# A graph network layer on Trainium2: other rules for when gathers are issued, in six stretches of the edge loop

## The chip, the core and the metric

The kernel runs on one core of a Trainium2 chip. A core has five engines, each with its own instruction queue: TensorE (PE in the profile; its weight loads are PEld), VectorE (DVE), ScalarE (ACT), GpSimd (POOL) and SyncE (SP). They meet only at semaphores. PE writes to the accumulators (PSUM), DVE and ACT take results from there, and DMA transfers move data between the device's memory and the on-chip memory. A gather here is an indirect DMA that POOL issues: it reads 128 row numbers and fetches 128 rows of 256 floats.

The metric is device time in microseconds (us); the shorter, the better. Beside the timed runs there is one profiled execution, with a record of every instruction.

## The reference

Nodes N = 6250 with D = 256 features, E = 206250 edges sorted by target, 64 features and one polarity per edge. Cut to what matters:

```python
h = relu(layernorm(x))
e = relu(raw @ W_e1.T + b_e1) @ W_e2.T + b_e2          # per edge
edge_emb = (e * (clip(edge_attr[:, 0:1], 0, 1) + 0.01)) @ W_le.T + b_le
msg  = relu(h[src] + edge_emb)
aggr = segment_sum(msg, dst, num_segments=6250)
o = (h + aggr) @ W_g1.T + b_g1
o = layernorm(o) * ln_g + ln_b
x = x + relu(o) @ W_g2.T + b_g2
```

## The kernel before

The matrices W_e2 and W_le are multiplied once into `wc_s`, so an edge needs two matmul layers. The kernel first makes `hb_d`, the normalised node rows plus b_le, in the device's memory. Then one long loop, written out instruction by instruction in this order (a manual schedule, nothing is moved by a planner), goes over the edges.

The edges are cut in tiles of 128. Two tiles are a **unit** (806 units, index `u`), four tiles a block, two blocks (four units) a **pair** (202 pairs). Six blocks are a group with one accumulator `pd` for the sums. For unit u:

- `edge_part(u)` (matmuls of L255): the second layer on PE into a PSUM tile `pz`, one of 7; DVE adds the bias into `msg` (L260).
- `whole(u)`: DVE multiplies by the edge's polarity and adds the gathered row into the gather's own buffer `hg` (L530, two instructions per unit); ACT takes the relu (L532).
- once per pair, when u % 4 is 1, `turn_of`: the first layer of a later pair (L233 on PE, L241 on ACT), then `sums` (`add_up`, L540): PE adds the finished `hg` of a pair into `pd` with 0/1 matrices `sel`, and frees their buffers; then the next load of edge features on SP.

There are 16 `hg` buffers of one unit. Gathers can't start before `hb_d` is written, so the loop begins with PE 22 units ahead: `made`, the number of units that went through `whole`, stands `LEAD - u // SHRINK` units behind u, 22 at the start and 1 at the end. When a group is complete, ACT copies `pd` (L546) and the work on the nodes follows in small pieces that `due` puts between the units (L161 to L188, L591 to L613).

What sets the order of the gathers: at each unit, after `forward(u)`, `ask` lets the number of asked units grow to `4 * summed + 12` plus 1, 2, 3 or 4, by the unit's place in the pair. For each new unit DVE copies its two columns of row numbers from `src_s` into a small tile `idx` (L500), then POOL gets the two gathers (L511). A gather waits for its `idx` copy, for the sums that free its buffer, and for the gather eight before it to have landed. The first 16 units are asked before the loop; on DVE their copies stand behind the two instructions that clip the polarities (L410, L411) and ahead of the cast of `dst_f` (L642).

Of the kernel before, what the change touches and what calls it, by code (L numbers as in the profile page):

```python
# [9 lines left out]
F32 = mybir.dt.float32  # L10
I32 = mybir.dt.int32
# [6 lines left out]
P = 128  # L18
# [10 lines left out]
S = 4  # L29
L = 6  # L30
W = 32
# [10 lines left out]
SHRINK = 36  # L42
HG = 16
TURN = 1
CH = 4
AHEAD = 10
assert DEG * N == E and NF * GE + S * P >= E
# [2 lines left out]
def group_of(b):  # L50
    return b // L


def blocks_of(g):
    return range(g * L, min((g + 1) * L, NB))
# [9 lines left out]
def groups_of(w):  # L65
    return [g for g in range(NG) if w in windows_of(g)]


def chunks():

    t = 0
    while t < NW:
        n = min(CH, N // P - t)
        if n <= 0:
# [17 lines left out]
def gnn_kernel(ctx: ExitStack, tc: tile.TileContext, x, src_c, dst_c, dst_r, pol_c, raw_t, w_e1t, w_e2,  # L92
               w_let, w_g1t, w_g2t, vec_c, row_v, x_t, out):
    nc = tc.nc

    const = ctx.enter_context(tc.tile_pool(name="const", bufs=1))
# [16 lines left out]
    wc_s = const.tile([P, 2, D], F32, name="wc_s")  # L113
    bc_s = const.tile([P, 2, D], F32, name="bc_s")
    src_s = const.tile([P, NT], I32, name="src_s")
# [82 lines left out]
    NU = 2 * NB  # L198
    fast = ExitStack()
    fast.enter_context(tc.manual_schedule())  # L200
    with fast:
# [8 lines left out]
        raw, sel, e1, hg, msg, ms = {}, {}, {}, {}, {}, {}  # L210

        pd = psd.tile([P, 2, D], F32, name="pd")

        def ps():
            return psz.tile([P, 2, D], F32, name="pz")
# [28 lines left out]
        def plain(u):  # L244

            return u < LEAD and u % 3 == 1

        def edge_part(u):

            b, v = divmod(u, 2)  # L250
            pz = ps()
            for i in range(2):
                k = (2 * v + i) * P
                for c in range(2):
                    nc.tensor.matmul(pz[:, i, :], e1[b][:, c, k:k + P], wc_s[:, c, :], start=c == 0, stop=c == 1)  # L255
            msg[u] = msg_p.tile([P, 2, D], F32, name="msg")
            if plain(u):
                nc.scalar.activation(msg[u], pz, AF.Copy)
            else:
                nc.vector.tensor_add(msg[u], pz, bc_s)  # L260
            if v == 1:
                e1.pop(b)

        sums = lambda: None

        def turn_of(q):

            if q + 2 < NP:
                first_layer(q + 2)
            sums()  # L270
            load_pair(q + 4)

        def forward(u):

            edge_part(u)
            if u % 4 == TURN:
                turn_of(u // 4)
# [30 lines left out]
        with tc.tile_pool(name="p1", bufs=4) as p1, tc.tile_pool(name="p1x", bufs=11) as p1x:  # L308
# [4 lines left out]
            def load_rows(k, halves=1):  # L313
                if k < len(parts):
                    t0, p, t = parts[k]
                    xts[k] = p1x.tile([P, CH, D], F32, name="xt")
                    h = t // halves
# [4 lines left out]
            def stats(k, i0, i1):  # L322
                t0, p, t = parts[k]
                if i0 == 0:
                    mvs[k] = p1.tile([P, CH, 2], F32, name="mvx")
                for i in range(i0, min(i1, t)):
                    row_stats(p1, p, 1, lambda _: xts[k][:p, i, :], mvs[k][:, i:i + 1, :])

            def root(k):
                t0, p, t = parts[k]  # L330
                nc.scalar.activation(rs_s[:p, t0:t0 + t], mvs[k][:p, :t, 1], AF.Sqrt, bias=eps_t[:p])

            def nodes_out(k):
# [6 lines left out]
                for i in range(t):  # L340
                    nc.scalar.activation(xt[:p, i, :], xt[:p, i, :], AF.Relu, bias=nm_s[:p, t0 + i:t0 + i + 1],  # L341
                                         scale=rs_s[:p, t0 + i:t0 + i + 1])
                hb = p1.tile([P, CH, D], F32, name="hb")
                for i in range(t):
# [40 lines left out]
            for k in range(len(parts) + 1):  # L385
# [9 lines left out]
                if k < len(parts):  # L395
                    stats(k, 2, CH)
                    root(k)
# [3 lines left out]
                for _ in range((k > 0) + (k > 2 and k % 3 > 0)):  # L401
                    u = next(units, None)
# [82 lines left out]


        with tc.tile_pool(name="hg", bufs=HG) as hg_p, tc.tile_pool(name="ms", bufs=5) as ms_p, \
                tc.tile_pool(name="sel2", bufs=9) as sel2_p, tc.tile_pool(name="nd", bufs=3) as nd, tc.tile_pool(name="idx", bufs=HG) as idx_p:
            idx = {}
            asked = 0  # L490
            got = 0
            made = 0
            summed = 0

            def ask(last):

                nonlocal asked
                while asked < min(NU, last):
                    idx[asked] = idx_p.tile([P, 2], I32, name="idx")
                    nc.vector.tensor_copy(idx[asked], src_s[:, 2 * asked:2 * asked + 2])  # L500
                    asked += 1
                gathers()

            def gathers():
                nonlocal got
                while got < asked:
                    u = got
                    got += 1
                    hg[u] = hg_p.tile([P, 2, D], F32, name="hg")
                    for i in range(2):  # L510
                        nc.gpsimd.indirect_dma_start(  # L511
                            out=hg[u][:, i, :], out_offset=None, in_=hb_d,
                            in_offset=bass.IndirectOffsetOnAxis(ap=idx[u][:, i:i + 1], axis=0))

            def select(g):

# [7 lines left out]
            def whole(u):  # L524

                m = msg.pop(u)
                if plain(u):
                    nc.vector.tensor_add(m, m, bc_s)
                for i in range(2):
                    nc.vector.scalar_tensor_tensor(hg[u][:, i, :], m[:, i, :], pol_s[:, 2 * u + i:2 * u + i + 1],  # L530
                                                   hg[u][:, i, :], op0=ALU.mult, op1=ALU.add)
                nc.scalar.activation(hg[u], hg[u], AF.Relu)  # L532

            def add_up(b):

                g = group_of(b)
                k = b - g * L
                for j in range(S):
                    m = hg[2 * b + j // 2]
                    nc.tensor.matmul(pd[j * W:(j + 1) * W, g % 2, :], sel[g][:, k * S + j, :], m[:, j % 2, :],  # L540
                                     start=k == 0, stop=b == blocks_of(g)[-1])
                hg.pop(2 * b)
                hg.pop(2 * b + 1)
                if b == blocks_of(g)[-1]:
                    ms[g] = ms_p.tile([P, D], F32, name="ms")
                    nc.scalar.activation(ms[g], pd[:, g % 2, :], AF.Copy)  # L546
                    sel.pop(g)
                    for w in range(NW):
                        if groups_of(w)[-1] == g:
                            late.pop(w)()  # L550
                        elif groups_of(w)[-1] == g + 1 < NG - 1:
                            late[w] = node_work(w)

            def add_pairs(last=False):

                nonlocal summed
                while summed < NP and min(4 * summed + 4, NU) < made + last:
                    for b in (2 * summed, 2 * summed + 1):
                        if b < NB:
                            add_up(b)  # L560
                            if b % L == 0 and group_of(b) + 2 < NG:
                                at(now + 2, lambda g=group_of(b) + 2: select(g))
                    summed += 1
# [3 lines left out]
            now = 0  # L567
# [65 lines left out]
            def due():  # L633

                fns = todo.pop(now, deque())
                if fns:
                    fns.popleft()()
                if fns:
                    todo.setdefault(now + 1, deque()).extendleft(reversed(fns))

            ask(HG)
            nc.vector.tensor_copy(dst_f, dst_f.bitcast(I32))  # L642
            sums = add_pairs
            for i, fn in enumerate((first_rows, rows_of_edges, lambda: select(0), lambda: select(1), row_numbers,
# [6 lines left out]
            for u in range(LEAD, NU):  # L651
                now = u
                forward(u)

                ask(4 * summed + HG - 4 + (u - TURN) % 4 + 1)
                while made < u + 1 - max(LEAST, LEAD - u // SHRINK):
                    whole(made)
                    made += 1
                due()
                if u == NU - 10:  # L660
                    for w in range(NW):
                        if groups_of(w)[-1] == NG - 1:
                            late[w] = node_work(w, True)
                if u == LEAD + 60:
                    flag = nc.values_load(bad_i[0:1, 0:1], min_val=0, max_val=3 * P)
# [4 lines left out]
            while todo:  # L670
                now = min(todo)
# [169 lines left out]
```

## Time and profile before

Three runs: 2218.32 us median (2217.36 to 2218.54).

| what | us |
|---|---|
| profiled execution | 2216.99 |
| its span, first to last instruction | 2215.3 |
| PE busy | 2190.5 |
| POOL busy, of it 1612 gathers of L511 | 1647.5, 1611.8 |
| DVE busy, of it 806 copies of L500 | 1535.6, 155.1 |
| ACT busy | 1064.2 |
| first gather starts, last gather starts (from the span's start) | 67.87, 2185.32 |

A row of the costliest groups has the line, the engine, the operation, the output and the inputs by the program's names, how often, then the busy time and the mean of one in ns, then the idle time of the engine just ahead of these instructions with what ended most of it. The view of waits has one row per pair of waiter and reason: the total, how often, the longest. A reason is the event that came last before the start, so a row names what finished last, which need not be what held the engine. "issue" is time in which the engine waited for nothing that the profile shows. In the timeline a line has the start, the duration, the engine, and in brackets the idle time before it. A gather's duration on POOL is that of its issue; the data lands later.

### The profile page before, as it was taken

Reading aid. Unit: us, or ns where it says so; the run is one execution under the profiler, and the core shown is the slowest. Engines: PE = TensorE matmul, PEld = TensorE weight load, DVE = VectorE, ACT = ScalarE, POOL = GpSimd, SP = SyncE. Lnnn points to the kernel's source line nnn. Section 1 sums busy time; section 2 is a strip of 40 time slices with the busy share of each in tenths; the row PEclk is TensorE's granted clock in tenths of the full one; section 3 lists DMA queues with packets and bytes.
Section 4 is the critical chain, followed back from the end, with each engine's and each line's share of the span. In section 5 each row is a group of like instructions: output and inputs, shape, how many; then the busy total and the mean of one; then the engine's idle time right before and its main releaser. Section 6 shows DMA issues by size and latency. Waiting matters only on the chain.

```text
span 2215.3 us, 35590 instructions
## 1 busy us (share of the span) xinstructions
PE 2190.5 (99%) x12360; PEld 1583.1 (71%) x12360; DVE 1535.6 (69%) x4083; ACT 1064.2 (48%) x1895; POOL 1647.5 (74%) x1674
## 2 busy tenths in 40 slices
PE   8999999999999999999999999999999999999997
PEld 6667777777777777777777776777777777777775
DVE  7786667677676666667667666766676667666766
ACT  7444454444444444444444445454444444454443
POOL 5777777777777777777777777777777777777773
PEclk9999999999999999999999999999999999999999
DMA  9444554444444444544444444444344344444442
GB/s 307 149 135 121 152 145 132 132 133 141 148 135 126 138 146 129 154 131 136 141 143 129 150 127 142 133 145 136 115 146 146 118 130 147 140 141 130 138 135 61
DMA packets 156083, 309.23 MB, mean 140 GB/s; under 512 B 33183, under 2 KB 77944, under 8 KB 155896
## 3 DMA queue, kind: packets, MB, share of 16 engines
q0 software_dynamic: 77376, 211.39, 32.2%
q1 hardware_dynamic: 77384, 92.24, 13.3%
q10 hardware_dynamic: 1136, 3.27, 0.4%
q8 instruction: 98, 1.61, 0.3%
q14 instruction: 89, 0.73, 0.1%
HBM read 293.92 MB, written 12.85 MB: 138 GB/s over the span
## 4 chain that ended last, share of the span: by engine, by line
PE 94%; DMA 2%; DVE 1%; issue 1%; ACT 0%; POOL 0%; SPq 0%; POOLq 0%; DVEq 0%; ACTq 0%
PE pz L255 62%; PE pz L233 17%; PE pd L540 9%; PE pz L611 3%; PE pz L183 2%; PE pz L161 2%; DMA hg<-hb_d,idx 1%; PE pz L173 0%; DVE hg L530 0%; POOL hg L511 0%; DMA raw<-in_raw_t_dram 0%; ACT e L241 0%; DVE msg L260 0%; DMA wle_s<-in_w_let_dram 0%; ACT hg L532 0%
## 5 line engine op out<-in xcount | busy, mean ns | idle before, releaser
L511 POOL DMA_INDIRECT hg<-hb_d,idx x1612 | 1611.8, 1000 | 512.6 <-issue 195.0
L255 PE MATMUL pz<-wc_s,e 128*128 128x256 f32 x6448 | 1479.1, 383 | 2.3 <-DVE msg L260 2.3
L255 PEld LDWEIGHTS pz<-wc_s,e 128*128 128x128 f32 x6448 | 1202.1, 190 | 239.2 <-issue 46.1
L532 ACT ACTIVATE hg<-hg 128x512 f32<-128x512 f32 x806 | 511.2, 634 | 1009.9 <-DVE hg L530 1005.4
L260 DVE TENSOR_TENSOR msg<-pz,bc_s 128x512 f32<-128x512 f32 x799 | 550.5, 689 | 601.2 <-PE pz L255 598.5
L530 DVE SCALAR_TENSOR_TENSOR hg<-msg,pol_s,hg 128x256 f32<-128x256 f32 x1612 | 707.2, 480 | 20.9 <-DMA hg<-hb_d,idx 19.6
L241 ACT ACTIVATE e<-pz,vecs 128x512 f32<-128x512 f32 x799 | 483.2, 686 | 97.3 <-PE pz L233 96.2
L233 PE MATMUL pz<-raw,we_s 64*128 64x512 f32 x1612 | 403.2, 617 | 5.5 <-DMA we_s<-in_w_e1t_dram 5.0
L233 PEld LDWEIGHTS pz<-raw,we_s 64*128 64x128 f32 x1612 | 139.8, 186 | 167.7 <-issue 135.2
L540 PE MATMUL pd<-hg,sel 128*32 128x256 f32 x3224 | 215.0, 385 | 4.1 <-ACT ms L546 4.1
L540 PEld LDWEIGHTS pd<-hg,sel 128*32 128x32 f32 x3224 | 84.4, 109 | 187.7 <-issue 134.8
L500 DVE COPY idx<-src_s 128x2 int32<-128x2 int32 x806 | 155.1, 197 | 0.0
L611 PEld LDWEIGHTS pz<-s,ms 128*128 128x128 f32 x560 | 70.1, 192 | 5.2 <-ACT ms L546 1.7
L611 PE MATMUL pz<-s,ms 128*128 128x128 f32 (+1 forms) x560 | 70.9, 275 | 1.7 <-ACT ms L546 1.5
L520 DVE TENSOR_TENSOR sel<-iota_w,rel 128x768 f32<-128x768 f32 x68 | 64.0, 941 | 0.0
L345 POOL TENSOR_TENSOR hb<-xt,rows_b 128x256 f32<-128x256 f32 (+1 forms) x49 | 34.2, 729 | 25.3 <-ACT xt L341 17.1
L183 PE MATMUL pz<-wg_s,nT 128*128 128x256 f32 (+1 forms) x196 | 50.3, 380 | 0.0
L161 PE MATMUL pz<-wg_s,hT 128*128 128x256 f32 (+1 forms) x196 | 50.1, 379 | 0.0
L601 DVE TENSOR_TENSOR hT<-hT,stb 128x256 f32<-128x256 f32 (+1 forms) x98 | 41.3, 421 | 1.7
L183 PEld LDWEIGHTS pz<-wg_s,nT 128*128 128x128 f32 (+1 forms) x196 | 36.9, 190 | 5.8 <-PE pd L540 0.4
L161 PEld LDWEIGHTS pz<-wg_s,hT 128*128 128x128 f32 (+1 forms) x196 | 37.1, 190 | 5.1
L176 ACT ACTIVATE nT<-pz,vecs 128x128 f32<-128x128 f32 (+1 forms) x98 | 38.8, 446 | 0.6 <-PE pz L173 0.6
(77 smaller groups left out, 359.4 us busy)
## 6 DMA issues: line engine op xcount, KB each, us to landing
raw<-in_raw_t_dram SPq DMA_DIRECT2D x202, 256.0 KB, 4.5
hg<-hb_d,idx POOLq DMA_INDIRECT x1612
stb<-st_d SPq DMA_DIRECT2D x49, 128.0 KB
hb_d<-hb SPq DMA_DIRECT2D x12, 512.0 KB
xt<-in_x_dram SPq DMA_DIRECT2D x48, 128.0 KB
hT<-in_x_t_dram SPq DMA_DIRECT2D x48, 128.0 KB, 4.0
out_dram<-ot SPq DMA_DIRECT2D x48, 128.0 KB, 2.0
xt<-in_x_dram SPq DMA_DIRECT2D x11, 512.0 KB, 8.9
```

The lines of the kernel that those rows point to most:

```text
L161: nc.tensor.matmul(ph[:n, 0, :], aT[:, c, :n], wg1_s[:, c, :], start=c == 0, stop=c == 1)
L183: nc.tensor.matmul(po[:n, 0, :], nT[:, c, :n], wg2_s[:, c, :], start=c == 0, stop=c == 1)
L233: nc.tensor.matmul(pe[s, c], we1_s[s * F:(s + 1) * F, c * P:(c + 1) * P], raw[q][s * F:(s + 1) * F, :], start=True, stop=True)
L241: nc.scalar.activation(e1[b][:, c, :], pe[s, c], AF.Relu, bias=be1_s[:, c:c + 1])
L255: nc.tensor.matmul(pz[:, i, :], e1[b][:, c, k:k + P], wc_s[:, c, :], start=c == 0, stop=c == 1)
L260: nc.vector.tensor_add(msg[u], pz, bc_s)
L500: nc.vector.tensor_copy(idx[asked], src_s[:, 2 * asked:2 * asked + 2])
L511: nc.gpsimd.indirect_dma_start(out=hg[u][:, i, :], out_offset=None, in_=hb_d, in_offset=bass.IndirectOffsetOnAxis(ap=idx[u][:, i:i + 1], a ...
L530: nc.vector.scalar_tensor_tensor(hg[u][:, i, :], m[:, i, :], pol_s[:, 2 * u + i:2 * u + i + 1], hg[u][:, i, :], op0=ALU.mult, op1=ALU.add)
L532: nc.scalar.activation(hg[u], hg[u], AF.Relu)
L540: nc.tensor.matmul(pd[j * W:(j + 1) * W, g % 2, :], sel[g][:, k * S + j, :], m[:, j % 2, :], start=k == 0, stop=b == blocks_of(g)[-1])
L611: nc.tensor.matmul(pa[:, c, :n], ms[g][:, c * P:(c + 1) * P], box["sel2"][i][:, :n], start=i == 0, stop=i == len(gs) - 1)
```

## The change

A table `STEPS` cuts the loop into six stretches by pair number (below 37, 70, 103, 136, 169, and the rest). A row has: how far the gathers may be asked at each of the four places in a pair; how many units back lies the unit whose matmuls the first gather of a call waits for (None: no such wait); whether at the first place it waits for the last sums instead; the columns of an idle memset on POOL (0: none) and for every how many units it is issued; and whether second gathers wait for the first half of the same unit's matmuls.

The copies `idx` are gone in all stretches: the gathers read their row numbers straight from `src_s`. The memsets write a tile `idle_t` that nobody reads. `edge_part` and `add_up` keep the matmuls that the gathers may wait for. The gathers now wait for: eight gathers back, their buffer, and what the table says. The stretch is chosen by the current unit; the units asked in it are some 12 to 16 units past the last summed one. The order of the instructions on PE, ACT and SP is the same as before; on DVE it is the same but for the copies.

```diff
@@ -42,6 +42,18 @@
+STEPS = (
+    (37, (1, 2, 3, 4), 0, False, 0, 1, True),
+    (70, (4, 4, 4, 4), None, False, 400, 1, False),
+    (103, (4, 4, 4, 4), None, False, 800, 4, False),
+    (136, (2, 2, 4, 4), 0, True, 0, 1, False),
+    (169, (4, 4, 4, 4), None, False, 1280, 4, False),
+    (999, (4, 4, 4, 4), 0, True, 0, 1, False),
+)
@@ -252,7 +264,8 @@
             for i in range(2):
                 k = (2 * v + i) * P
                 for c in range(2):
-                    nc.tensor.matmul(pz[:, i, :], e1[b][:, c, k:k + P], wc_s[:, c, :], start=c == 0, stop=c == 1)
+                    z = nc.tensor.matmul(pz[:, i, :], e1[b][:, c, k:k + P], wc_s[:, c, :], start=c == 0, stop=c == 1)
+                zs.setdefault(u, []).append(z)
             msg[u] = msg_p.tile([P, 2, D], F32, name="msg")
             if plain(u):
                 nc.scalar.activation(msg[u], pz, AF.Copy)
@@ -261,6 +274,9 @@
             if v == 1:
                 e1.pop(b)
 
+        zs = {}
+        last_sums = None
+        idle_t = const.tile([P, 1280], F32, name="idle_t")
         sums = lambda: None
 
         def turn_of(q):
@@ -485,32 +501,34 @@
 
 
         with tc.tile_pool(name="hg", bufs=HG) as hg_p, tc.tile_pool(name="ms", bufs=5) as ms_p, \
-                tc.tile_pool(name="sel2", bufs=9) as sel2_p, tc.tile_pool(name="nd", bufs=3) as nd, tc.tile_pool(name="idx", bufs=HG) as idx_p:
-            idx = {}
-            asked = 0
+                tc.tile_pool(name="sel2", bufs=9) as sel2_p, tc.tile_pool(name="nd", bufs=3) as nd:
             got = 0
             made = 0
             summed = 0
 
-            def ask(last):
-
-                nonlocal asked
-                while asked < min(NU, last):
-                    idx[asked] = idx_p.tile([P, 2], I32, name="idx")
-                    nc.vector.tensor_copy(idx[asked], src_s[:, 2 * asked:2 * asked + 2])
-                    asked += 1
-                gathers()
-
-            def gathers():
+            def step(q):
+                return next(s[1:] for s in STEPS if q < s[0])
+
+            def gathers(last, behind=None, half=None):
+
                 nonlocal got
-                while got < asked:
+                while got < min(NU, last):
+                    cols, every = step(now // 4)[3:5]
+                    if cols and got % every == 0:
+                        nc.gpsimd.memset(idle_t[:, :cols], 0.0)
                     u = got
                     got += 1
                     hg[u] = hg_p.tile([P, 2, D], F32, name="hg")
                     for i in range(2):
-                        nc.gpsimd.indirect_dma_start(
+                        g = nc.gpsimd.indirect_dma_start(
                             out=hg[u][:, i, :], out_offset=None, in_=hb_d,
-                            in_offset=bass.IndirectOffsetOnAxis(ap=idx[u][:, i:i + 1], axis=0))
+                            in_offset=bass.IndirectOffsetOnAxis(ap=src_s[:, 2 * u + i:2 * u + i + 1], axis=0))
+                        if i and half is not None:
+                            behind = half
+                        if behind is not None:
+                            tc.add_manual_dep(g.ins, behind.ins.name, mybir.DependencyInfo(
+                                mybir.DependencyClass.Sync, mybir.DependencyReason.DATA), reason="gathers in step with PE")
+                            behind = None
 
             def select(g):
 
@@ -533,11 +551,12 @@
 
             def add_up(b):
 
+                nonlocal last_sums
                 g = group_of(b)
                 k = b - g * L
                 for j in range(S):
                     m = hg[2 * b + j // 2]
-                    nc.tensor.matmul(pd[j * W:(j + 1) * W, g % 2, :], sel[g][:, k * S + j, :], m[:, j % 2, :],
+                    last_sums = nc.tensor.matmul(pd[j * W:(j + 1) * W, g % 2, :], sel[g][:, k * S + j, :], m[:, j % 2, :],
                                      start=k == 0, stop=b == blocks_of(g)[-1])
                 hg.pop(2 * b)
                 hg.pop(2 * b + 1)
@@ -638,7 +657,7 @@
                 if fns:
                     todo.setdefault(now + 1, deque()).extendleft(reversed(fns))
 
-            ask(HG)
+            gathers(HG)
             nc.vector.tensor_copy(dst_f, dst_f.bitcast(I32))
             sums = add_pairs
             for i, fn in enumerate((first_rows, rows_of_edges, lambda: select(0), lambda: select(1), row_numbers,
@@ -652,7 +671,10 @@
                 now = u
                 forward(u)
 
-                ask(4 * summed + HG - 4 + (u - TURN) % 4 + 1)
+                ask, ahead, by_sums, _, _, halves = step(u // 4)
+                k = (u - TURN) % 4
+                behind = last_sums if by_sums and k == 0 and last_sums else None if ahead is None else zs[u - ahead][1]
+                gathers(4 * summed + HG - 4 + ask[k], behind, zs[u - ahead][0] if halves else None)
                 while made < u + 1 - max(LEAST, LEAD - u // SHRINK):
                     whole(made)
                     made += 1
```

## The prediction

> **What bounds the kernel now.** I read the page first: the shares of the engines, the chain that ended last, and the costliest groups.
>
> ```profile
> PE 2190.5 (99%) x12360; PEld 1583.1 (71%) x12360; DVE 1535.6 (69%) x4083; ACT 1064.2 (48%) x1895; POOL 1647.5 (74%) x1674
> ...
> PE 94%; DMA 2%; DVE 1%; issue 1%; ACT 0%; POOL 0%; SPq 0%; POOLq 0%; DVEq 0%; ACTq 0%
> ...
> L511 POOL DMA_INDIRECT hg<-hb_d,idx x1612 | 1611.8, 1000 | 512.6 <-issue 195.0
> ```
>
> PE is on the path for 94% of the span. POOL looks free at 74%, but its row says otherwise: 512.6 us of idle time over 1612 gathers is 0.318 us before each. So I asked for POOL's own waits in the first part of the loop, 68 to 1300 us (reason: total us, times, longest):
>
> ```profile
> POOL hg L511 <- issue: 121.0, 397, 0.3
> POOL hg L511 <- DVE hg L530: 50.3, 165, 0.3
> POOL hg L511 <- DVE idx L500: 25.1, 64, 6.0
> POOL hg L511 <- ACT hg L532: 18.6, 61, 0.3
> ```
>
> Every pause but one is 0.3 us, whatever engine is named. That is the fixed gap of one gather after another; the named engine only happened to finish inside it. The one exception is the 6.0 us ahead of the first gather. In the timeline of POOL and of DVE around 1014 us:
>
> ```profile
> 1014.23 0.95 POOL L511 DMA_INDIRECT hg<-hb_d,idx  x1 [0.30 <-PE pz L233]
> 1015.49 0.94 POOL L511 DMA_INDIRECT hg<-hb_d,idx  x1 [0.31 <-DVE hg L530]
> 1016.73 0.95 POOL L511 DMA_INDIRECT hg<-hb_d,idx  x1 [0.30 <-issue]
> 1017.98 0.95 POOL L511 DMA_INDIRECT hg<-hb_d,idx  x1 [0.30 <-issue]
> ```
>
> ```profile
> 1014.42 0.16 DVE L500 COPY idx<-src_s 128x2 int32<-128x2 int32 x1
> 1018.47 0.16 DVE L500 COPY idx<-src_s 128x2 int32<-128x2 int32 x1
> ```
>
> Gathers start 1.25 us apart with nothing between them. Over the loop the mean spacing is 1000 + 304 = 1304 ns, so a pair of blocks (8 gathers) takes POOL 10.43 us. PE takes (2186 - 68) / 196 pairs = 10.8 us. POOL therefore has 0.4 us of room per pair, and the shrinking lead (one unit of 2.7 us every nine pairs) takes 0.3 of it. In the whole run POOL stands still beyond the 0.30 us for only 16 us, all after 1300 us. PE bounds the kernel, and POOL is a second bound directly behind it.
>
> How far behind is the time from a gather's end on POOL to the DVE instruction of L530 that uses it, taken from the starts and durations of both in the trace: means of 7.5 us at gather 278, 12.6 at 551, 16.7 at 817, 20.7 at 1095, 17.8 at 1361, 16.6 at the last. The shortest, 1.7 us, is at the start, where DVE does wait for the data, so some 1.8 us is the landing itself.
>
> **The change, part by part.** *Copies of indices.* 806 copies leave DVE (155.1 us busy). DVE is 69% busy and stands behind PE, so that alone is worth nothing. Two things follow at the start: the first gather waited for the copies, which stood behind the two polarity instructions until 67.42; the transfers that it also waits for had been passed at 64.7, so with its 0.3 us it can start at about 65.0 instead of 67.87, 2.9 us sooner. PE's early stalls (1.3 us for the cast of dst_f behind the copies, 2.6 us at 113 and 125 us, about 1.4 in small pieces) can go: up to 5 us, if PE stays the bound.
>
> A rule of the Trainium skill speaks for more (SBUF — State Buffer, "Who interferes with whom"): a copy on DVE may run in a mode that locks GpSimd out of the port pair they share, and a gather's descriptors are written through it. By that rule the gathers would lose up to the copies' 155 us. By the rows above a gather with a copy inside it takes the same 0.94 to 0.95 us; over the trace the 577 gathers that overlap a copy and no other suspect average 966 ns, the 802 that overlap none 985. I take the row: no gain, and keep the rule as a rival.
>
> *Waits on PE.* In stretches 1, 4 and 6 the first gather of a call waits for edge matmuls of the current unit or for the last sums. The buffer it writes already waits for the sums of a pair earlier, so the wait is new by at most two or three units (5 to 8 us). POOL is further behind its buffers than that: DVE uses unit v while buffers are allowed up to about 11 units (29 us) ahead, and the lead is under 21. Behind the waiting gather stand all later gathers, but the wait is over when POOL gets to it. The wait of the second gather for the first half of the same unit's matmuls is older than the wait of the first gather: nothing. Cost 0; if POOL had caught up, up to 8 us once, hidden by the lead. Asking for four units at once gives permission sooner to an engine that isn't waiting for it: 0.
>
> *Memsets on POOL.* These are the cost. By the program's order there are 137 of 400 columns (one per unit, gathers 278 to 551), 34 of 800 (one per four units, 552 to 817) and 34 of 1280 (1096 to 1361). Each stands in POOL's queue ahead of gathers. The nearest rows are memsets at the very start of POOL's timeline:
>
> ```profile
> 0.32 0.10 POOL L832 MEMSET const-float32-0.0<- 128x1 f32 x1 [0.32 <-issue]
> 0.35 0.10 POOL L832 MEMSET const-float32-1.0<- 128x1 f32 x1
> ...
> 0.81 0.20 POOL masks.py:197 MEMSET ident<- 128x128 f32 x1 [0.29 <-POOLq L832]
> ```
>
> One column records 104 ns but the next starts 0.03 us later; 128 columns record 204. The slope is 100/127 = 0.79 ns a column, so a memset holds POOL for 0.35, 0.66 and 1.04 us, and in sum 48 + 22 + 35 = 105 us. The skill (GPSIMD Engine Reference, "Elementwise — side-by-side cycle accounting") gives a light loop 1.03 cycles an element at 1.2 GHz, 0.86 ns, an estimate of 0.37, 0.72 and 1.13 us, in sum 114. A slope over 127 columns carried to 1280 is the weaker of the two; I take 0.37, 0.71, 1.10: 51 + 24 + 37 = 112 us (the row alone would end 7 us lower).
>
> What no row shows is how a memset meets the 0.30 us ahead of a gather. Bounds: it vanishes in that gap as far as it can (0.07, 0.41, 0.80: 10 + 14 + 27 = 51 us), or it comes on top (112 us), or it brings a second gap (205 x 0.30 more: 174 us). The gap is the same whether a gather waits for one semaphore or four, and the semaphore instructions of the next gather are seen running during the present one; so it looks like work of POOL's own cores, which a memset can't share. I take 112.
>
> *What hides it.* Slack up to a gather = its lead, less 1.8 for landing, plus 2.9 from the earlier start, plus POOL's standstill up to there (0, 0, 10, and 16 at the end), plus about 4 for what DVE and PE absorb (DVE waited 15.6 us for gathers before 150 us and PE stalled 2.6 at its units; the seven PSUM buffers cover some 6 us at most; so 0 to 6).
> - gather 551: 51 - (12.6 - 1.8 + 2.9 + 4 = 17.7) = 33 us late
> - gather 817: 75 - (16.7 + 5.1 = 21.8) = 53
> - gather 1361: 112 - (17.8 + 5.1 + 10 = 32.9) = 79
> - last: 112 - (16.6 + 5.1 + 16 = 37.7) = 74
>
> The largest decides, since a delay of PE isn't won back: 79 us. What is late next: DVE at L530, behind it the additions of L260, then PE for PSUM buffers and at the sums. The 5 us of early stalls do not add, because POOL, not PE, sets the end. The profiled execution took 2217.0 (span 2215.3 and 1.7 around it), so 2296 for it; the median of the runs is 1.3 above, so **2297**.
>
> **Rivals.** *The gap swallows memsets* (51 us on POOL): 51 - 33 = 18, time 2237. For it: the gap could be the sequencer's, free while a memset runs. Against it: the semaphore instructions seen running early. *Each memset brings its own gap* (174 us): 174 - 33 = 141, 2359. For it: POOL's gap comes between any two gathers; against it: the additions of L345 follow each other without one. *Faster*: the copies did stretch the gathers after all. It decides from 79 / 1361 = 0.058 us less per gather, that is when nearly all of the 54 ns between the mean (1000) and the median (946) goes; then PE is the bound again without its early stalls, 2213. Against it stands the comparison of 966 and 985 ns, and that the longest gathers fall on the instruction of L520 (mean 1242 ns), which stays.
>
> **How the numbers follow.** Memsets on top: 0.57, own range 2270 to 2325. Swallowed: 0.17 (2228 to 2262). Own gap: 0.15 (2325 to 2375). Faster: 0.07. No change, within the 0.2% that a measurement here can tell: 0.02. Beyond 2375: 0.02. Leaving out both ends to 0.2 gives 2232 to 2362. Slower: 0.57 + 0.17 + 0.15 + 0.02 = 0.91.
>
> **What would show it.** A memset group of 205 rows of about 0.4, 0.7 and 1.1 us; POOL's starts one unit apart 2.6 + 0.37 us in stretch 2. DVE waits for the gathers' DMA in stretches 2, 3 and 5 and hardly elsewhere, and PE gets waits for DVE and ACT there, with some 33, 20 and 26 us in each. Median gather still 946 ns. It is wrong if the gathers' mean falls clearly under 1000 ns, if the 0.30 us shrinks behind a memset, or if stretches 4 and 6 also lose time, which would be the waits on PE.

## The result, and the profile after

The changed kernel takes 2280.69 us (median of 4 runs, 2277.57 to 2282.42); the kernel before, beside it, 2217.84 (4 runs, 2216.39 to 2218.54). The ratio is 1.0279, with a 95% interval of 1.0266 to 1.0292: slower by 63 us. The profiled execution took 2282.42, its span is 2280.7 (65.4 more than before).

The page of the changed kernel, the shares of the engines and two of the costliest groups:

```profile
PE 2220.2 (97%) x12360; PEld 1593.2 (70%) x12360; DVE 1516.0 (66%) x3277; ACT 1059.5 (46%) x1895; POOL 1764.7 (77%) x1879
...
L523 POOL DMA_INDIRECT hg<-hb_d,src_s x1612 | 1601.1, 993 | 465.6 <-issue 357.1
...
L548 DVE SCALAR_TENSOR_TENSOR hg<-msg,pol_s,hg 128x256 f32<-128x256 f32 x1612 | 738.8, 480 | 443.0 <-DMA hg<-hb_d,src_s 436.2
```

POOL shows 77%, so it seems still to have a quarter of its time free. The row of L523 (the gathers, L511 before) says what that quarter is: 465.6 us over 1612 gathers, 0.29 us ahead of each. The third row is the new fact: DVE now waits 436.2 us for gathered data. The waits of DVE say the same more fully, first the kernel before, then the changed one (reason: total us, times, longest):

```profile
DVE msg L260 <- PE pz L255: 598.5, 522, 4.9
DVE hg L530 <- DMA hg<-hb_d,idx: 19.6, 28, 1.8
```

```profile
DVE hg L548 <- DMA hg<-hb_d,src_s: 436.2, 571, 3.7
...
DVE msg L273 <- PE pz L267: 263.3, 237, 3.7
```

Before, DVE waited for PE 522 times and for gathers 28 times. Now it waits for gathers 571 times: the bound has gone from PE to POOL for part of the loop. For which part, the view of several stretches at once tells (length, busy time of PE, PEld, DVE, ACT and POOL with the number of instructions, granted clock, share of DMA, GB/s). The rows are stretches 1, 2, 5 and 6 of the changed kernel:

```profile
68.00:430.00 362.00, 357.19 (x2005) 255.45 (x2004) 250.76 (x533) 170.60 (x303) 277.44 (x280) 1.00 0.45 134
430.00:824.00 394.00, 378.42 (x2082) 267.68 (x2081) 249.12 (x525) 170.13 (x303) 331.08 (x404) 0.99 0.43 127
...
1545.00:1918.00 373.00, 363.86 (x2043) 262.81 (x2040) 243.75 (x511) 169.37 (x301) 297.84 (x295) 0.99 0.43 128
1918.00:2252.00 334.00, 333.19 (x1880) 241.13 (x1879) 227.84 (x494) 157.33 (x279) 256.14 (x258) 1.00 0.45 134
```

In the kernel before, the same stretch of the loop (its gathers ran from 430 to 787 us) had PE busy throughout and POOL at 274/357 = 77%:

```profile
430.00:787.00 357.00, 357.00 (x2032) 259.08 (x2024) 246.63 (x656) 170.31 (x302) 273.82 (x274) 1.00 0.46 137
```

In the changed kernel POOL's share goes to 331/394 = 84% in stretch 2, and PE stands still for 15.6 us; in stretch 6, without memsets, PE is full again. For the loss itself I compare, from the starts in both traces, when DVE uses the same gather (its "use"). How long the uses of each stretch take:

| stretch (gathers up to) | before, us | after, us | difference | forecast |
|---|---|---|---|---|
| 1 (278) | 368.4 | 367.5 | -0.9 | 0 |
| 2 (552), 400 columns | 361.9 | 397.0 | +35.1 | 33 |
| 3 (818), 800 columns | 350.9 | 361.9 | +11.0 | 20 |
| 4 (1096) | 370.3 | 369.0 | -1.3 | 0 |
| 5 (1362), 1280 columns | 350.5 | 369.6 | +19.1 | 26 |
| 6 (1611) | 323.2 | 324.9 | +1.7 | 0 |

The three stretches with memsets lose 65.2 us together, the three without them -0.5. What a memset costs POOL is read from its groups, with shapes kept apart (count, busy us, mean ns), and from its timeline:

```profile
L518 POOL MEMSET idle_t<- 128x400 f32 x137 | 61.8, 451 | 0.0
L518 POOL MEMSET idle_t<- 128x1280 f32 x34 | 40.2, 1183 | 0.0
...
L518 POOL MEMSET idle_t<- 128x800 f32 x34 | 26.6, 784 | 0.0
```

```profile
600.27 0.94 POOL L523 DMA_INDIRECT hg<-hb_d,src_s  x1 [0.30 <-issue]
601.20 0.46 POOL L518 MEMSET idle_t<- 128x400 f32 x1
601.82 0.95 POOL L523 DMA_INDIRECT hg<-hb_d,src_s  x1 [0.17 <-ACT ms L565]
603.08 1.20 POOL L523 DMA_INDIRECT hg<-hb_d,src_s  x1 [0.30 <-issue]
```

A memset begins the moment the gather ends, and after it only 0.17 us pass, not 0.30. So its recorded time is not its price. The price is how far it moves the next gather: from a gather's end to the next one's start it takes 0.304 to 0.305 us without a memset, and in the median 0.611, 0.944 and 1.344 with 400, 800 and 1280 columns. That is 0.307, 0.640 and 1.040 us on top, a straight line of 0.833 ns a column less 26 ns. At all three widths it is the recorded mean (451, 784, 1183 ns) less 0.144 us: that much of a memset the gap takes in, and no more of a wider one. With 137, 34 and 34 of them: 42.1 + 21.8 + 35.4 = 99.2 us.

POOL's own balance from the first gather to the last closes: start 2.7 us earlier, memsets +99.3, standstill gone (-16), gathers 10.7 shorter in all; the sum, 70, is how much later the last gather starts (2255.14 against 2185.32). It closes because POOL never stands still in the changed kernel: no gap between two gathers without a memset is longer than 0.308 us. So nothing that the gathers were made to wait for held them there, and nothing that only slows PE could have moved them. From the start of the last gather the end comes 4.4 us sooner than before, and that gives the 65.4 of the span.

### The profile page after: what moved, and what is told of

Its sections match the earlier page's. It is cut to its first block, busy times and chain, and to the rows that moved or that the text cites. A ratio compares the mean times of both kernels' runs of the same rounds, so it can differ in the third digit from the quotient of the medians.

```text
span 2280.7 us, 34186 instructions
## 1 busy us (share of the span) xinstructions
PE 2220.2 (97%) x12360; PEld 1593.2 (70%) x12360; DVE 1516.0 (66%) x3277; ACT 1059.5 (46%) x1895; POOL 1764.7 (77%) x1879
## 5 line engine op out<-in xcount | busy, mean ns | idle before, releaser
L523 POOL DMA_INDIRECT hg<-hb_d,src_s x1612 | 1601.1, 993 | 465.6 <-issue 357.1
L548 DVE SCALAR_TENSOR_TENSOR hg<-msg,pol_s,hg 128x256 f32<-128x256 f32 x1612 | 738.8, 480 | 443.0 <-DMA hg<-hb_d,src_s 436.2
L245 PE MATMUL pz<-raw,we_s 64*128 64x512 f32 x1612 | 408.2, 618 | 4.9 <-DMA we_s<-in_w_e1t_dram 4.9
L559 PE MATMUL pd<-hg,sel 128*32 128x256 f32 x3224 | 221.8, 386 | 15.5 <-ACT hg L550 7.8
L518 POOL MEMSET idle_t<- 128x400 f32 (+2 forms) x205 | 128.7, 628 | 0.1
L630 PEld LDWEIGHTS pz<-s,ms 128*128 128x128 f32 x560 | 72.1, 196 | 14.5 <-ACT ms L565 11.1
L538 DVE TENSOR_TENSOR sel<-iota_w,rel 128x768 f32<-128x768 f32 x68 | 63.9, 939 | 0.0
L610 DVE TENSOR_SCALAR s<-iota_p,rowid 128x128 f32<-128x128 f32 x140 | 40.6, 414 | 0.0
```

Source lines behind the costliest of these rows:

```text
L245: nc.tensor.matmul(pe[s, c], we1_s[s * F:(s + 1) * F, c * P:(c + 1) * P], raw[q][s * F:(s + 1) * F, :], start=True, stop=True)
L518: nc.gpsimd.memset(idle_t[:, :cols], 0.0)
L523: g = nc.gpsimd.indirect_dma_start(out=hg[u][:, i, :], out_offset=None, in_=hb_d, in_offset=bass.IndirectOffsetOnAxis(ap=src_s[:, 2 * u + ...
L559: last_sums = nc.tensor.matmul(pd[j * W:(j + 1) * W, g % 2, :], sel[g][:, k * S + j, :], m[:, j % 2, :], start=k == 0, stop=b == blocks_of ...
L630: nc.tensor.matmul(pa[:, c, :n], ms[g][:, c * P:(c + 1) * P], box["sel2"][i][:, :n], start=i == 0, stop=i == len(gs) - 1)
```

## The experiments

The theory: memsets take POOL's time one by one, the lead of the gathers (the time from a gather's end on POOL to its use) hides some of it, and nothing else in the change moves the end. The rivals: the new waits, the other asking rules or the missing copies cost or win something; losses of one stretch come back in another. e1 to e4 were run side by side (there the kernel before took 2219.26, 19 runs).

**Everything but the memsets (e1).** All columns of the table are 0.

```diff
-    (70, (4, 4, 4, 4), None, False, 400, 1, False),
+    (70, (4, 4, 4, 4), None, False, 0, 1, False),
```

The rows of 800 and 1280 columns are changed in the same way.

> The changed kernel with all idle columns set to 0; waits on PE, asking rules and the missing copies stay. Theory (POOL's memsets are the whole loss): about 2213 us, 5 under before, since PE is the bound again and loses its early stalls. Rival (the waits on PE and the four-at-once asking cost time themselves): 2225 or more, with stretches 1, 4 and 6 longer.

Measured 2217.32 us (13 runs), ratio 0.9993, interval 0.9984 to 1.0001. Its waits of DVE:

```profile
DVE msg L273 <- PE pz L267: 659.4, 542, 5.3
DVE hg L548 <- DMA hg<-hb_d,src_s: 19.3, 28, 2.4
```

DVE waits for PE again, and for gathers 28 times as before. Waits on PE, waits for sums, other asking rules and 806 missing copies together change nothing that can be measured. The 2213 that I gave for PE as bound without its early stalls wasn't reached: the uses run 1.5 us ahead at gather 60, and 1.4 behind from gather 200 on. (A second execution of the kernel before, in e10, is 1.2 behind there too, so 1.4 is within what executions differ by.) Between 68 and 150 us PE still waits 3.6 us in sum, against 5.3 before.

**The memsets alone (e2).** The kernel before with the same memsets in front of the same units, but for one of 400 columns: its asking rules stay, so the stretch of memsets ends one unit earlier (204 memsets, not 205). Its copies stay too.

```diff
+IDLE = ((37, 0, 1), (70, 400, 1), (103, 800, 4), (136, 0, 1), (169, 1280, 4), (999, 0, 1))
...
+                    cols, every = next(s[1:] for s in IDLE if now // 4 < s[0])
+                    if cols and got % every == 0:
+                        nc.gpsimd.memset(idle_t[:, :cols], 0.0)
```

> The kernel before with the same 205 memsets put ahead of the same gathers and nothing else; copies and asking as before. Theory: the memsets carry the loss, 2283 us (before plus 63, plus 3 for the later start of the first gather). Rival (rules for waits and asking carry part of it): 2260 or less.

Measured 2284.15 us, ratio 1.0294 (1.0278 to 1.0310). The page: the share of each engine in the chain that ended last, the gathers, the memsets:

```profile
PE 70%; DMA 11%; DVE 6%; POOL 5%; ACT 4%; issue 4%; POOLq 0%; ACTq 0%; DVEq 0%
...
L516 POOL DMA_INDIRECT hg<-hb_d,idx x1612 | 1600.6, 993 | 468.2 <-issue 250.4
...
L511 POOL MEMSET idle_t<- 128x400 f32 (+2 forms) x204 | 128.3, 629 | 0.1
```

PE falls from 94% of the chain to 70%; gathers' data, DVE and POOL come in its place. (In the changed kernel the chain breaks off at once, so it can't be read there.) The memsets carry the whole loss. Two more things follow. With copies the mean gather is 993 ns here, and without them 993 in the changed kernel: the copies have no hold on the gathers that shows. (Without memsets a small difference is left: 996 ns in e1, 1000 and 1001 in the two traces of the kernel before. Over the loop that is 6 to 8 us of POOL's time, which a kernel bound by PE doesn't show.) And the other parts of the change, the early start of 2.7 us among them, do not add to the loss: 2284 without them, 2281 with them.

**Only the 400 columns (e4)**, in stretch 2.

```diff
-    (103, (4, 4, 4, 4), None, False, 800, 4, False),
+    (103, (4, 4, 4, 4), None, False, 0, 1, False),
...
-    (169, (4, 4, 4, 4), None, False, 1280, 4, False),
+    (169, (4, 4, 4, 4), None, False, 0, 1, False),
```

> The changed kernel with the memsets of 400 columns alone (stretch 2). They hold POOL for 137 x 0.307 = 42 us. Theory (a queue with a lead: only what exceeds the lead at that place is lost): about 33 us over before less the 0 to 2 us that is won at the end, 2249 to 2251. Rival (each us of memset costs its share, 63 of 99): 27 us, 2245. DVE should wait for gathers from 500 to 830 us and the lead should grow again afterwards.

Measured 2243.95 us, ratio 1.0109 (1.0093 to 1.0124). The time alone doesn't tell theory from rival: it lies 6 us under the theory, at the rival's number. The trace does tell. Against the kernel before, uses are 29.1 us late at gather 551, and from gather 817 on 27.6 to 27.8 late to the end, so no more than 1.5 us is won back. Its waits of DVE between 430 and 824 us:

```profile
DVE hg L548 <- DMA hg<-hb_d,src_s: 115.5, 141, 3.7
DVE msg L273 <- PE pz L267: 22.1, 17, 3.4
```

Between 1545 and 1918 us no wait for a gather is left. The lead grows again, from 3.2 us at gather 551 to 19.3 at 1361: the lead returns, the lost time doesn't. The missing 6 us are in the gathers of stretch 2: their mean is 986 ns here and 1007.6 in the changed kernel, 274 x 0.021 = 5.8 us. Why they differ is not settled, so the time agrees with the rival by chance as far as this shows.

**Only the 1280 columns (e3)**, in stretch 5.

```diff
-    (70, (4, 4, 4, 4), None, False, 400, 1, False),
-    (103, (4, 4, 4, 4), None, False, 800, 4, False),
+    (70, (4, 4, 4, 4), None, False, 0, 1, False),
+    (103, (4, 4, 4, 4), None, False, 0, 1, False),
```

> The changed kernel with the memsets of 1280 columns alone (stretch 5). They hold POOL for 34 x 1.040 = 35 us. Theory: the lead there (17.8 us), the standstill of POOL up to there (10) and the earlier start cover about 31, so 2214 to 2222. Rival (each us costs its share): 22 us, 2240.

Measured 2226.78 us, ratio 1.0032 (1.0020 to 1.0044). Its waits of DVE between 1545 and 1918 us:

```profile
DVE msg L273 <- PE pz L267: 60.3, 52, 3.4
DVE hg L548 <- DMA hg<-hb_d,src_s: 58.7, 78, 3.2
```

Here the lead is shown at work. It is 19.4 us when the memsets begin and 3.0 when they end, and of 35.4 us only 7.4 reach the uses (from 2.0 us ahead of the kernel before at gather 1095 to 5.4 behind at 1361; 7.7 at the end). The same memsets cost 18.5 us between the same two gathers in the changed kernel, where two stretches had used up the lead before. The result is 5 us above the theory's range. That range left out the 1.8 us of landing that the forecast takes off the lead, and reckoned from 2218 where the kernel before, timed beside it, took 2219.3. With both the sum is 35.4 - (17.8 - 1.8 + 2.9 + 10) = 6.5 us, so 2225.8.

**One column (e5), and twice the columns (e6, on two chips).** The three widths are 1, 1, 1 in one kernel, and 800, 1600, 2560 in the other (for that, `idle_t` has 2560 columns). The row of stretch 2 in both:

```diff
-    (70, (4, 4, 4, 4), None, False, 400, 1, False),
+    (70, (4, 4, 4, 4), None, False, 1, 1, False),
```

```diff
-    (70, (4, 4, 4, 4), None, False, 400, 1, False),
+    (70, (4, 4, 4, 4), None, False, 800, 1, False),
```

> The changed kernel with the same 205 memsets at the same places, each of one column. Theory: behind a memset a gather starts 0.165 us after its recorded end, and one column records about 0.12, so the 0.304 us gap holds it all: no loss, as without memsets, 2217 us. Rival (each memset costs a fixed gap of its own): 205 x 0.3 = 61 us on POOL, about 2245.

> The changed kernel with twice the columns in every memset (800, 1600, 2560). At 0.833 ns a column less 26 ns they hold POOL for 0.640, 1.307, 2.107 us, 204 us in sum, 105 more than in the changed kernel. Theory (POOL alone sets the pace once its lead is gone, each further us is one us): 2281 plus 105 = 2386. Rival (loss in proportion to the memsets, 63 x 2): 2344. Rival (a waiting PE loses clock): over 2400 with a granted clock well under 0.99.

> The kernel with twice the columns once more, since in the first run of it PE paused for nothing in the program. Theory (POOL alone sets the pace once its lead is gone): 105 us over the changed kernel, 2386, a ratio of 1.075 to before. Rival (in proportion to the memsets): 2344, ratio 1.056. Rival (a waiting PE loses clock): over 2400.

These runs, and the next three, were on two chips where the kernel before itself takes 2591 us (below), so their totals say nothing on the theory; what holds is the spacing on POOL. One column, then the double width, in the timeline of POOL:

```profile
501.11 0.96 POOL L523 DMA_INDIRECT hg<-hb_d,src_s  x1 [0.30 <-issue]
502.07 0.11 POOL L518 MEMSET idle_t<- 128x1 f32 x1
502.37 0.95 POOL L523 DMA_INDIRECT hg<-hb_d,src_s  x1 [0.19 <-issue]
```

```profile
600.59 0.95 POOL L523 DMA_INDIRECT hg<-hb_d,src_s  x1 [0.30 <-issue]
601.54 0.78 POOL L518 MEMSET idle_t<- 128x800 f32 x1
602.49 0.95 POOL L523 DMA_INDIRECT hg<-hb_d,src_s  x1 [0.17 <-PE pz L245]
```

One column records 0.11 us and moves the next gather by nothing: in stretch 2 it takes 305 ns in the median from gather to gather, where without a memset it takes 304 to 305. The doubled memsets add 0.640, 1.307 and 2.107 us, the straight line of above continued (0.833 x 1600 - 26 = 1307). The line would be below nothing at one column; there it is cut off at nothing, because the gap covers what such a memset takes.

Total times: one column 2642.40 us, ratio 1.0204 (1.0165 to 1.0244); double width 2576.57, 0.9960 (0.9940 to 0.9979), and on the second chip 2580.94, 0.9969 (0.9953 to 0.9985). The total that the theory gives for double width was neither met nor refuted, since most of the time there over 2219 us is in the kernel before as well.

**No copies alone (e7, on two chips), and more lead (e8).** The kernel before without its copies; and that with `LEAD` 26 and `SHRINK` 31.

```diff
-                    idx[asked] = idx_p.tile([P, 2], I32, name="idx")
-                    nc.vector.tensor_copy(idx[asked], src_s[:, 2 * asked:2 * asked + 2])
...
-                            in_offset=bass.IndirectOffsetOnAxis(ap=idx[u][:, i:i + 1], axis=0))
+                            in_offset=bass.IndirectOffsetOnAxis(ap=src_s[:, 2 * u + i:2 * u + i + 1], axis=0))
```

```diff
-LEAD = 22
+LEAD = 26
...
-SHRINK = 36
+SHRINK = 31
```

> The kernel before with nothing changed but the row numbers read straight from src_s, no copies on DVE. Theory: the time stays within 0.2% of before or up to 3 us under it by the earlier first gather; mean gather 990 to 1005 ns. Rival (the copies locked POOL out of the shared port): mean gather near 950 ns. The row of the gathers tells them apart, the time can't, since PE bounds it.

> The kernel before without the copies and nothing else, once more for the same reason. Theory: within 0.2% of before or up to 3 us under it; mean gather 990 to 1005 ns. Rival (the copies locked POOL out): mean gather near 950 ns. A second rival from the disturbed run: the missing copies cost time by themselves, 4% as there.

> No copies, no memsets, and LEAD 26 with SHRINK 31 in place of 22 and 36: PE stands four units further ahead of the gathers at the start. Theory (in the first 150 us POOL is the bound and costs PE its early stalls): 2 to 4 us less than without it, 2213 to 2216, and no waits of DVE for gathers after 100 us. Rival (the start is bound by PE and the transfers): no change.

Measured without copies 2695.36 us, ratio 1.0406 (1.0372 to 1.0440), and on the second chip 2703.56, 1.0422 (1.0367 to 1.0477); with more lead 2727.86, 1.0529 (1.0498 to 1.0559). All miss. The gathers are not at fault (means of 983 to 990 ns, median 946). Without copies, on the first of these chips, the waits of PE begin with

```profile
PE pz L255 <- issue: 86.4, 102, 2.3
PE pz L608 <- issue: 56.2, 60, 3.4
```

that is, with pauses in which PE waits for nothing that the trace shows. The kernel before, on the undisturbed chip, has no such row. So both questions stay open: e1 has the copies gone too and loses nothing, but copies alone, and a larger lead, were not measured on an undisturbed chip.

**Both kernels once more on another chip (e9, e10)**, to see whether the disturbance belongs to the kernels.

> The changed kernel itself, timed again beside the kernel before, for the chip on which the kernel with twice the columns was no slower than before. Theory (where PE stands still for reasons outside the program, POOL has room and the memsets are hidden): on such a chip 2570 to 2620 us, a ratio of 0.99 to 1.01. Rival (the memsets cost their 63 us there too): 2654, ratio 1.024. On a chip like the first ones: 2281, ratio 1.028.

> The kernel before, for its trace on the same chip. Theory: PE's pauses of over 0.7 us with nothing waited for sum to some 320 us, 100 less than the 420 of the kernel without copies there. Rival: the same 420, and the difference of 105 us lies in the clock.

This chip was like the first: the changed kernel 2278.72 us against 2219.20 (7 runs), ratio 1.0262 (1.0245 to 1.0279), and its uses late by 33.0, 45.2, 60.7 and 61.9 us at gathers 551, 817, 1361 and the last. That repeats the result with the same course. The kernel before gave one time, 2219.77. As neither chip of the disturbed kind came, their question is as open as before.

## Why the prediction was right, and where its sizes were off

The forecast was 2297 us; 2281 came. The mechanism is the one forecast: memsets on top of the gap, the lead covers a part, PE gets the rest as delay that isn't won back. The size was 16 us too large, 79 us of loss for 63. Point by point:

- **Bound.** PE first and POOL directly behind it: e2 shows that work on POOL alone makes POOL the bound.
- **Price of a memset.** Forecast 0.37, 0.71, 1.10 us, measured 0.307, 0.640, 1.040; in sum 99.2, not 112. This is the largest error, 13 us. I took the row's 105, raised towards the 114 of the page's rule (the Trainium skill, GPSIMD Engine Reference, "Elementwise — side-by-side cycle accounting": 1.03 cycles an element at 1.2 GHz, an estimate of 0.86 ns). The slope measured is 0.833 ns, 3% under that rule, but the fixed part that I added isn't paid: it lies in the gap.
- **The gap.** The memsets come on top of it to within 26 ns of their time by column. The rival in which it swallows memsets (51 us on POOL) and the one in which each brings a second gap (174 us) both fall: 0.307 stands against 0.07 and 0.67.
- **Copies worth nothing.** This was right. In stretch 1, where they are gone and there are no memsets, the mean gather is 1001.5 ns against 1001.6 before; in all undisturbed runs it is 1001.5 to 1005.0 there without copies and 1001.6 to 1008.2 with them. Counted plainly, 700 gathers of the kernel before overlap a copy (mean 998 ns) and 912 don't (1001). The rival that they stretch the gathers enough to matter (by some 50 ns) falls with these numbers, and on these small copies the rule of a shared port (the Trainium skill, SBUF — State Buffer, "Who interferes with whom") shows no such effect.
- **Waits on PE and asking rules: 0.** This was right, by e1, by stretches 4 and 6, which lose -1.3 and +1.7 us, and by POOL's gaps, none of which is over 0.308 us.
- **Earlier start 2.9, standstill 16.** Measured 2.7, and 16.0 used up wholly.
- **Early stalls of PE, up to 5 us.** Of 5.3 us of PE's waits between 68 and 150 us, 2.3 are left in the changed kernel and 3.6 in e1, and e1 is not measurably faster for it. As forecast, they don't add, since POOL sets the end.
- **Cushion of 4 us in DVE and PE.** It isn't there. Up to gather 1361 the slack, without it, is 17.8 - 1.8 + 2.9 + 10 = 28.9; measured is 99.3 - 8.4 (shorter gathers) - 60.3 = 30.6. Up to 551 it is 13.7 by forecast and 42.1 + 1.8 - 32.8 = 11.1 measured. The mean lead around a gather was too coarse a measure: the leads of gathers 1361 and 551 themselves, 19.4 and 10.3 us, with the start and the standstill as measured, give 30.7 and 11.2.
- **Gathers.** I held them at 1000 ns. They are 10.7 us shorter in sum, 8.4 of them up to gather 1361, most of it in stretches 3 and 5. The median stays 946. Copies are out as the cause: e2 has them and the same mean, 993. The traces show where most of it lies: in gathers that run beside the DVE instruction of L520 (L538 after), which makes the 0/1 matrices. Before, 107 gathers overlap it with a mean of 1242 ns, after, 98 with a mean of 1189, and that is 8 of the 10.7 us. Why they meet it less, no run shows.
- **Waits named as signs.** The memset groups and DVE's waits for gathers in stretches 2, 3 and 5 came (118.5, 109.2 and 85.0 us by the windows above). But DVE also waits 36.2 and 65.3 us in stretches 4 and 6, which lose nothing, so such a wait is not a loss by itself. And PE's waits in stretches 2, 3 and 5 are 14.2, 9.6 and 9.1 us, not 33, 20 and 26. Of the 65.4 us of span 29.7 stand in the profile as more busy time of PE for the same 12360 matmuls. Half clock can account for some 12 of it (an estimate: 32.6 us at half clock against 8.7 before, half of the difference); the rest is not explained.
- **Lateness** at gathers 551, 817, 1361 and the last: forecast 33, 53, 79, 74; measured 32.8, 43.1, 60.3, 62.7. So 79 became 60: 13 less for memsets (all lie before that point), 8 less for gathers, and 2 more because the slack was 2 smaller than forecast with its cushion.

That stretch 2 hits its 33 us is partly luck: memsets 9 us cheaper (42 for 51), but the slack 7 smaller (11 for 17.7) and the gathers 2 longer.

**A lower clock isn't the cause.** The changed kernel's granted clock is 0.993 (0.998 before); in stretches 2, 3 and 5 there are five windows of 3.4 to 6.8 us, 20.5 in all, at half clock, and before there is none between 76 and 2212 us. But e2, with practically the same memsets, has 0.996 and loses as much; e4 has 0.999, no half clock in the loop, and still loses its 28 us in stretch 2. And POOL, which sets the pace there, never stood still for PE.

## What to carry to other kernels

A queue engine can be full at 74% busy: divide its idle time by its instructions and look for a constant, 0.3 us here, before calling it free. Work put on such an engine costs what it moves the next instruction by, not its recorded duration, and is hidden only by the lead that it has over its consumers at that place, once: a lead spent in one stretch is missing in the next (the same 1280 columns cost 7 us with a full lead and 18 with a spent one). So follow lateness from consumer to consumer through the whole loop rather than comparing totals, as one total here (e4) agreed with the wrong account.

## What was not expected

- **Two chips on which the order of kernels turns.** On two of the four chips of the experiments the kernel before takes 2591 us. There twice the idle work is 0.3 to 0.4% faster than the kernel before and leaving out the copies is 4% slower, the same on both. The traces there show a granted clock of 0.92 to 0.96 and many pauses of PE with nothing waited for that the trace shows ("issue" in its waits): in sum 176 us with one column, 113 and 124 with double width, 207 and 218 without copies, 193 with more lead, and none in the kernel before on the first chip. The time at half clock goes with them: 348, 191 and 221, 375 and 407, and 438 us. Among these runs the kernel with the most work on POOL has the fewest pauses; that is an observation, not a cause. There is no trace of the kernel before on those chips, so what the pauses come from stays open.
- **Short drops to half clock** in the changed kernel on an undisturbed chip, as given above: 20.5 us in five windows. Each begins within 1.5 us of the end of a pause of PE of 1.9 to 3.7 us. They aren't the changed kernel's alone: e1, without memsets, has one too, at 159 us, just after a pause of 1.8.
- **A gap that a memset can enter but hardly use:** it starts at the gather's very end, and yet only 0.144 us of it, the same from 400 to 2560 columns, delays nothing.
